# Reordering the DMA issues of a fused attention and spline-FFN kernel: an earlier input load, block moves ahead of other transfers, and a second issuing engine

## The chip, the cores and the metric

The kernel runs on one core of a Trainium2 chip. The metric is the device time of one execution in microseconds (us). Three runs of the kernel before gave 541.97, 543.44 and 547.85 us; their median, 543.44 us, is the time before. Engines are called PE (matrix multiplication), DVE (vector), ACT (scalar, activations), POOL (GpSimd) and SP (which here does nothing but issue DMAs).

## The reference

Everything is float32. `x` has 4 batches of 512 tokens of 512 features. A layer norm is shared by an attention of 16 heads (head size 32, ALiBi bias, causal mask) and by a gated FFN whose three weight matrices are dense samples of Catmull-Rom splines through a few control points.

```python
xn = _layernorm(x)
q, k, v = proj(xn, Wq, bq), proj(xn, Wk, bk), proj(xn, Wv, bv)
scores = einsum("bhqd,bhkd->bhqk", q, k) / sqrt(32) + alibi + causal_mask
attn = softmax(scores) @ v            # heads joined again, then @ Wo + bo
gate_w, up_w, down_w = (spline_reconstruct(cp) for cp in control_points)
inter = silu(xn @ gate_w.T) * (xn @ up_w.T)
out = x + attn + inter @ down_w.T
```

## The kernel before

The kernel has two stages. The first (to about 385 us) is the attention, with the preparation of the FFN's tables beside it; the second is the FFN, a sequence of plain steps that the change does not touch. The instruction order on each engine is the order in which the Python code writes it (`in_order`, L385), so the text of the main loop (L1104 to L1169) is the schedule.

**Units.** The attention is cut into 64 units `(b, hg, i)`: batch, group of four heads, query tile `i` of 128 queries. Four units with one `(b, hg)` are called a group here, numbered 0 to 15 (four groups a batch). Step `n` of the loop starts unit `n`; older units are in later phases. For a unit: PE makes the scores (L897); DVE adds the bias and finds minima (`minima`, L917); ACT takes exponentials with their sums (`exponentials`, L932); DVE takes reciprocals (L945) and POOL multiplies by them (`normalize`, L947).

**Turning the probabilities.** For the product with `v` the probabilities must lie with keys on partitions. Key tile 0 of query tiles 0 and 1 is transposed by PE (`turn`, L951). Everything else goes in two parts (`swap`, L963): DVE transposes 32x32 blocks into a tile `blocks0` or `blocks1` (L972), and then four DMAs, one for each 32 source partitions `a`, spread the blocks over partitions into one shared tile, called `moved` in the profile (`move`, L977 to L982). Query tile 1 has 4 moves of 64 KB, tile 2 4 of 192 KB, tile 3 4 of 256 KB. Tiles 1 and 3 share the buffer `blocks1` (`i % 2`): DVE can't write tile 3's blocks until tile 1's moves have landed, and not tile 1's of the next group until tile 3's have landed. `values` (L986) multiplies `moved` by `v` on PE (L1000), at step 3 of the next group; the next group's moves may not overwrite `moved` until that is done.

**Where the moves stand.** Within a step the order is: DVE and ACT work of the unit, the transposes of `swap`, spline-table arithmetic on DVE (`terms`, L1150), the lists `items[n]` and `small[n]` (projections, loads and so on, hung on a step by the code from L1022 to L1068), then the collected `moves` (L1157), then the deferred DMAs in `later` (`flush`, L1159), then table loads (L1163). At step 0 of a group the transposes of tile 2 (of the group that ended) come before the minima of the new tile 0 and 1, those of tile 3 after them; the moves of both come at the end of the step. Tile 1's are at step 3.

**Queues.** All DMAs but the table copies (POOL, L553) and a few rows of zeros are issued by SP, one after the other; SP waits in order. The framework gives the DMAs of SP and ACT eight completion semaphores in turn, so that a DMA also waits for the one eight before it to have landed.

**Other work on the queue.** `load_turned` (L806) loads the next batch's raw `x`, transposed, 1 MB, into one of two `xnT` buffers; it hangs on `items[at + 6]` (L1052), where `at` is the batch's first step. `norm_turned` (L810, DVE, L814) normalizes it in place from step `at + 8` on, with row statistics that come back through DRAM (`write_rows` L798, `read_rows` L804), and PE's `value` (L863) and projections (L827) need it from step `at + 10` on. `project_out` (L1026) spreads the output projection of the batch before: a load of `xT` into one of three `xt` buffers (L485, 256 KB) hangs on step `n - 2`, PE and DVE work on step `n` (L490, L497), and the result's store (L500) goes into `later`. `stepped` (L878) makes four small moves of `v` into `moved` (L884) once a batch.

Of the kernel before, what the change touches and what calls it, by code (L numbers as in the profile page):

```python
# [23 lines left out]
NB = D // P  # L24
# [376 lines left out]
def block_kernel(  # L401
# [18 lines left out]
    nc = tc.nc  # L420
# [52 lines left out]
    later = deque()  # L473

    def flush():
        while later:
            later.popleft()()

    def proj(b, r, pool, tag):

        xt = []

        def load():
            xt.append(xtp.tile([P, S], F32, name="xt"))
            nc.sync.dma_start(out=xt[0], in_=xT[b, r * P : (r + 1) * P, :])  # L485

        def go():
            ps = pool.tile([P, S], F32, name=tag)
            for c in range(NB):
                nc.tensor.matmul(  # L490
                    ps,
                    lhsT=wsb["o"][:, c, r * P : (r + 1) * P],
                    rhs=ctxT[b][:, c, :],
                    start=(c == 0),
                    stop=(c == NB - 1),
                )
            nc.vector.scalar_tensor_tensor(  # L497
                xt[0], ps, bocol[:, r : r + 1], xt[0], ALU.add, ALU.add
            )
            later.append(lambda: nc.sync.dma_start(out=mid[b][:, r], in_=xt[0]))  # L500

        return [load, go]
# [47 lines left out]
    def copy_rows(n):  # L550
        for _ in range(n):
            to, rows = copies.popleft()
            nc.gpsimd.dma_start(out=to, in_=rows)  # L553
# [31 lines left out]
    with ExitStack() as att:  # L585
# [216 lines left out]
        def read_rows(b):  # L802
            rows[b] = tp.tile([P, 2, S], F32, name="rows")
            nc.sync.dma_start(out=rows[b], in_=token[b].partition_broadcast(P))  # L804

        def load_turned(b):  # L806
            xnT[b] = xtp.tile([P, NB, S], F32, name="xnT", bufs=2)
            nc.sync.dma_start(out=xnT[b], in_=xn0[b].rearrange("(c p) s -> p c s", p=P))

        def norm_turned(b, t):  # L810
            at = slice(t * P, (t + 1) * P)
            for k, op in enumerate((ALU.subtract, ALU.mult)):
                own = rows[b][:, k, at].unsqueeze(1).to_broadcast([P, NB, P])
                nc.vector.tensor_tensor(xnT[b][:, :, at], xnT[b][:, :, at], own, op)  # L814
# [71 lines left out]
        units = [(b, hg, i) for b in range(B) for hg in range(NHG) for i in range(NB)]  # L886
# [76 lines left out]
        def swap(u):  # L963

            b, hg, i = u
            if i == 0:
                return lambda: None
            first = int(i < TURNED)
            at = slice(3 * i - 4 + first, 4 * i - 3)
            own = tp.tile([P, NB, i + 1 - first, NG, Q32], F32, name=f"blocks{i % 2}")  # L970
            for c in range(first, i + 1):
                nc.vector.transpose(  # L972
                    own[:, :, c - first].rearrange("p r j k -> p j r k"),
                    soft[u][0][:, :, c * P : (c + 1) * P].rearrange("p j (r k) -> p j r k", k=Q32),
                )

            def move():  # L977
                for a in range(NB):
                    nc.sync.dma_start(  # L979
                        out=blocks[:, a, at].rearrange("p s j k -> p (s j k)"),  # L980
                        in_=own[a * Q32 : (a + 1) * Q32].rearrange("p r s j k -> p r (s j k)"),
                    )  # L982

            return move
# [37 lines left out]
        items = {n: [] for n in range(len(units) + LAG)}  # L1022
# [3 lines left out]
        def project_out(b, spots):  # L1026
            for r, n in enumerate(spots):
                load, go = proj(b, r, *((ps_m, "mm") if n < len(units) else (ps_s, "s")))
                items[n - 2].append(load)
                (early if n % NB == NB - 1 else items)[n].append(go)  # L1030

        for b in range(B):
            at = 4 * NHG * b
            for hg in range(NHG):
                nb, nh = divmod(b * NHG + hg + 1, NHG)
                if nb < B:

                    items[at + 4 * hg - (b > 0 and hg == 1)].append(project("q", nb, nh))
                    items[at + 4 * hg + 1 + (b > 0 and hg == 1)].append(project("k", nb, nh))
            if b == 0:  # L1040
                items[0].pop()
                items[0], items[1] = items[1], []
                for n, t in ((1, 1), (2, 2), (3, 3)):
                    items[n].append(value(0, t))
            elif b < B - 1:
                project_out(b - 1, [at + n for n in (4, 5, 6, 7)])
            else:
                project_out(b - 1, [at + n for n in (10, 12, 14, 16)])
            if b + 1 < B:
                for t in range(NB):  # L1050
                    small[at + 8 + t].append(lambda b=b, t=t: norm_turned(b + 1, t))
                items[at + 6].append(lambda b=b: load_turned(b + 1))  # L1052
                small[at + 5].append(lambda b=b: write_rows(b + 1))
                items[at + 7].append(lambda b=b: read_rows(b + 1))
                for t, n in enumerate(((10, 11, 14, 15), (10, 11, 14, 15), (14, 18, 19, 22))[b]):
                    items[at + n].append(value(b + 1, t))
                for n, step in zip((1, 1, 2, 2, 3, 3, 3, 4, 4), stat_steps(b + 1)):
                    small[at + n].append(step)
                if b + 2 < B:
                    items[at + 11].append(lambda b=b: load_x(b + 2))  # L1060
        for b in range(B):
            at = 4 * NHG * b
# [41 lines left out]
        for n in range(len(units) + LAG):  # L1104
            u = units[n] if n < len(units) else None
            old = units[n - LAG] if n >= LAG else None
            if u and u[2] != 1:
                scores(u)
            moves = []
            if u and u[2] == 0:  # L1110
                if old and old[2] < TURNED:
                    turn(old)
                if n:
                    normalize(units[n - 1])
                    moves.append(swap(units[n - 2]))
                minima(u)
                minima(units[n + 1])
            else:
                if u and u[2] > 1:
                    minima(u, range(NG // 2))  # L1120
                if n <= len(units):
                    normalize(units[n - 1])
                if u and u[2] > 1:
                    minima(u, range(NG // 2, NG))
            for step in early[n]:
                step()
            keep_it = None
            if n % NB == NB - 1 and n >= NB + LAG:
                g = n // NB - 1
                keep_it = values(g // NHG, g % NHG)  # L1130
                exponentials(u, range(NG))
                keep_it()
            if old and old[2] < TURNED and not (u and u[2] == 0):
                turn(old)
            if u and not keep_it:
                exponentials(u, range(NG))
            if n % NB == 0 and n:
                if u is None:
                    moves.append(swap(units[n - 2]))
                moves.append(swap(units[n - 1]))  # L1140
            elif n % NB == NB - 1:
                moves.append(swap(units[n - 2]))
            assert n < 53 or done == len(terms)
            if n >= NB:
                credit = min(credit + TERMS[n % NB] - 0.3 * len(small[n]), 2.0)
            while done < len(terms) and credit > 0.0:
                cost, of, *term = terms[done]
                if of in due or of in fresh:
                    break
                nc.vector.tensor_tensor(*term)  # L1150
                done += 1
                credit -= cost
                if done in loads:
                    due[done] = loads[done]
            for step in (*items[n], *small[n]):
                step()
            for move in moves:  # L1157
                move()
            flush()  # L1159
            fresh = set()  # L1160
            if n % NB in (1, 2):
                for load in due.values():
                    load()  # L1163
                fresh = set(due)
                due.clear()
            if n >= 12:
                copy_rows(min(COPIES[n % NB], len(copies) - 2 * NB))
            if old:
                soft.pop(old)  # L1169
# [241 lines left out]
```

## Time and profile before

| | |
|---|---|
| median of three runs | 543.44 us (541.97 to 547.85) |
| profiled execution | 538.82 us |
| its span, first to last instruction | 537.0 us |
| mean granted PE clock | 0.974 |
| PE busy | 497.2 us (93%) |
| DVE / ACT / POOL busy | 366.8 / 267.7 / 255.2 us |
| moves of tile 1 / 2 / 3 | 64 each; 64 / 192 / 256 KB; median 3.1 / 3.7 / 4.8 us from issue to landing |

A row of the profile names the source line, the engine, the operation and the tiles as `out<-in`. "Idle before" is the time in which an engine did nothing just before the instruction, with the instruction or DMA whose end released it. In the timeline, `SPq` rows are DMA issues, and the second number is how long the issuing took. `PEclk` is the granted PE clock, 1.0 being full speed. The DMA share is the mean busy share of the 16 DMA engines.

### The profile page before, as it was taken

What the parts mean: (1) busy time and instruction counts of PE and PEld (TensorE: products, weight loads), DVE (VectorE), ACT (ScalarE), POOL (GpSimd) and SP (SyncE); (2) the same over time, 40 slices, a digit from 0 to 9 for tenths busy, and PEclk for the clock granted to TensorE, in tenths of its full rate; (3) what the DMA queues carried; (4) which work ended last, traced back from release to release, by engine and by line L of the source; (5) the groups of instructions that cost most, each with busy time, mean ns of one, the idle gap of its engine ahead of it and who ended that gap; (6) DMA issues with size and microseconds to landing.
All of it is one profiled execution on the core that took longest, in us unless ns stands there. A gap on an engine that the chain in (4) does not pass through costs nothing.

```text
span 537.0 us, 11697 instructions
## 1 busy us (share of the span) xinstructions
PE 497.2 (93%) x4092; PEld 240.0 (45%) x4092; DVE 366.8 (68%) x1023; ACT 267.7 (50%) x726; POOL 255.2 (48%) x441
## 2 busy tenths in 40 slices
PE   7999959998994999799998999978899999999997
PEld 5644414444441434344344444334334645746463
DVE  6069879879675997886887566684035584855836
ACT  2376646746361675544676756772214433624222
POOL 4025536848272974827567647673018233231310
PEclk9999979999997999799999999997999999999999
DMA  8925888979888787878868657886956566745344
GB/s 305 363 83 110 306 225 293 268 224 282 236 248 237 249 214 256 254 174 247 202 158 231 154 117 201 243 213 181 260 160 190 177 213 199 245 137 205 123 165 166
DMA packets 67522, 114.31 MB, mean 213 GB/s; under 512 B 10796, under 2 KB 29228, under 8 KB 66952
## 3 DMA queue, kind: packets, MB, share of 16 engines
q1 hardware_dynamic: 62600, 105.08, 66.6%
q0 software_dynamic: 4864, 8.49, 5.4%
q8 instruction: 32, 0.52, 0.4%
q14 instruction: 26, 0.21, 0.1%
HBM read 54.27 MB, written 23.70 MB: 145 GB/s over the span
## 4 chain that ended last, share of the span: by engine, by line
PE 59%; DMA 14%; DVE 14%; SPq 6%; issue 4%; ACT 2%; POOL 1%; DVEq 0%; ACTq 0%
PE mm L827 12%; PE g L568 9%; PE mm L863 6%; DMA moved<-blocks 6%; PE o L1283 6%; DVE blocks L972 5%; PE c L1000 5%; PE s L897 4%; SPq L979 4%; PE o L1229 4%; DVE p L917 4%; PE o L1300 3%; PE o L490 3%; PE mm L490 3%; DMA xt<-in_xT_dram 2%
## 5 line engine op out<-in xcount | busy, mean ns | idle before, releaser
L947 POOL TENSOR_SCALAR p<-p,inv 128x128 f32<-128x128 f32 (+3 forms) x256 | 155.6, 621 | 156.2 <-DVE inv L945 154.8
L932 ACT ACTIVATE p<-p,low 128x128 f32<-128x128 f32 (+3 forms) x256 | 140.4, 551 | 82.2 <-DVE low L917 77.9
L917 DVE CUSTOM_DVE_ANT_0 p<-s,dist 128x128 f32<-128x128 f32 (+3 forms) x256 | 109.9, 480 | 49.0 <-PE s L897 48.9
L972 DVE STREAM_TRANSPOSE blocks<-p 128x512 f32<-128x512 f32 x128 | 81.1, 681 | 27.5 <-DMA moved<-blocks 26.4
L1205 POOL COPY made<-inner 128x512 f32<-128x512 f32 x64 | 38.8, 635 | 104.1 <-DVE inner L1204 66.1
L863 PE MATMUL mm<-wv,xnT 128*128 128x512 f32 x128 | 62.7, 634 | 14.0 <-issue 13.0
L568 PE MATMUL g<-feat,wT 32*64 32x512 f32 x832 | 61.7, 592 | 0.0
L1197 ACT ACTIVATE act<-g 128x512 f32<-128x512 f32 x60 | 31.0, 602 | 58.9 <-PE g L568 58.6
L827 PE MATMUL mm<-xnT,wq 128*128 128x512 f32 (+1 forms) x136 | 57.9, 569 | 1.0 <-DVE xnT L814 0.7
L827 PE MATMUL mm<-xnT,wk 128*128 128x512 f32 (+1 forms) x136 | 58.1, 570 | 0.2 <-ACT xnT L778 0.2
L897 PE MATMUL s<-kT,qT 32*128 32x512 f32 (+3 forms) x512 | 52.1, 468 | 2.3 <-DVE low L917 2.2
L932 ACT ACTIVATION_READ_ACCUMULATOR p<-p,low 128x1 f32 x256 | 48.2, 188 | 0.0
L1000 PE MATMUL c<-moved,v 128*32 128x256 f32 (+2 forms) x512 | 34.2, 412 | 14.7 <-DMA xt<-in_xT_dram 5.7
L863 PEld LDWEIGHTS mm<-wv,xnT 128*128 128x128 f32 x128 | 24.6, 203 | 44.2 <-issue 39.6
L490 PE MATMUL mm<-ctxT,wo 128*128 128x512 f32 x88 | 39.7, 597 | 0.0
L1204 DVE TENSOR_TENSOR inner<-g,act 128x512 f32<-128x512 f32 x40 | 24.8, 683 | 21.7 <-PE g L568 10.7
L827 PEld LDWEIGHTS mm<-xnT,wk 128*128 128x128 f32 x136 | 25.5, 190 | 29.5 <-issue 27.5
L568 PEld LDWEIGHTS g<-feat,wT 32*64 32x64 f32 x832 | 28.9, 131 | 21.1 <-issue 9.9
L897 PEld LDWEIGHTS s<-kT,qT 32*128 32x128 f32 x512 | 21.4, 184 | 35.3 <-issue 16.4
L553 POOL DMA_DIRECT2D table<-samples x64 | 36.7, 579 | 0.0
L827 PEld LDWEIGHTS mm<-xnT,wq 128*128 128x128 f32 x136 | 24.8, 190 | 24.5 <-issue 22.0
L1283 PE MATMUL o<-inner,dRM 32*64 32x512 f32 x512 | 34.9, 588 | 0.0
(114 smaller groups left out, 588.8 us busy)
## 6 DMA issues: line engine op xcount, KB each, us to landing
moved<-blocks SPq DMA_DIRECT2D x64, 256.0 KB, 4.8
moved<-blocks SPq DMA_DIRECT2D x64, 192.0 KB, 3.7
feat<-table SPq DMA_DIRECT2D x16, 512.0 KB, 4.7
inner<-made SPq DMA_DIRECT2D x32, 256.0 KB, 4.5
table<-samples POOLq DMA_DIRECT2D x64, 88.0 KB, 4.8
xp<-in_xp_dram SPq DMA_DIRECT2D x16, 256.0 KB, 4.6
feat<-in_coef_dram SPq DMA_DIRECT2D x8, 512.0 KB, 5.4
feat<-in_rowpts_dram SPq DMA_DIRECT2D x8, 512.0 KB, 8.0
```

Source lines behind the costliest of these rows:

```text
L490: nc.tensor.matmul(ps, lhsT=wsb["o"][:, c, r * P : (r + 1) * P], rhs=ctxT[b][:, c, :], start=(c == 0), stop=(c == NB - 1),)
L568: nc.tensor.matmul(ps[k][cols, :], lhsT=wT[rows, q, 2 * w + part, cols], rhs=feat[b][rows, q, part, :], start=(part == 0), stop=(part == 1),)
L827: nc.tensor.matmul(ps[0][:, tokens], lhsT=wsb[name][:, c, hg * P : (hg + 1) * P], rhs=xnT[b][:, c, tokens], start=(c == 0), stop=(c == NB ...
L863: nc.tensor.matmul(ps[0], lhsT=xnT[b][:, c, t * P : (t + 1) * P], rhs=wsb["v"][:, c, :], start=(c == 0), stop=(c == NB - 1),)
L897: nc.tensor.matmul(banks[b, hg][j][:, at : at + (k + 1) * P], lhsT=qk[b, hg, "q"][rows, k * P : (k + 1) * P], rhs=qk[b, hg, "k"][rows, : ( ...
L917: nc.vector.tensor_tensor_reduce(out=p[:, j, :nk], in0=ps[j], in1=own, scale=-SLOPES[hg * NG + j], scalar=BIG, op0=ALU.add, op1=ALU.min, a ...
L932: nc.scalar.activation(p[:, j, :nk], p[:, j, :nk], AF.Exp, bias=low[:, j : j + 1], scale=-1.0, accum_out=total[:, j : j + 1],)
L947: nc.gpsimd.tensor_scalar(p[:, j, :nk], p[:, j, :nk], inv[:, j : j + 1], 1.0, ALU.mult, ALU.mult)
L972: nc.vector.transpose(own[:, :, c - first].rearrange("p r j k -> p j r k"), soft[u][0][:, :, c * P : (c + 1) * P].rearrange("p j (r k) -> ...
L1000: nc.tensor.matmul(ps[j * HD : (j + 1) * HD, to], lhsT=v(j), rhs=part(j), start=(c == 0), stop=(c == NB),)
L1205: nc.gpsimd.tensor_copy(made[:, k], four[:, k])
L1283: nc.tensor.matmul(sums[b][r][cols, :], lhsT=dR[rows, a, cols], rhs=o[rows, :], start=(a == 0), stop=False,)
```

## The change

Four edits in the attention's schedule; no arithmetic changes, and PE, DVE and POOL carry the same instructions in the same order.

1. `load_turned(b + 1)` hangs on step `at + 2` (`at + 3` for the first batch) and not on `at + 6`.
2. The load of `xT` in `project_out` goes into `later`, so that it is issued after the moves of its step.
3. At step 0 of a group the moves of tile 2 are issued at once, ahead of whatever DMAs the step's `items` issue.
4. Of tile 3's four moves, those with `a` = 1 and 3 are issued by ACT; SP keeps 0 and 2. On ACT they stand behind the exponentials of tile 0 and the query projection's copy (L839) and ahead of the exponentials of tile 1.

```diff
@@ swap
             def move():
                 for a in range(NB):
-                    nc.sync.dma_start(
+                    queue = nc.scalar if i == NB - 1 and a % 2 else nc.sync
+                    queue.dma_start(
                         out=blocks[:, a, at].rearrange("p s j k -> p (s j k)"),
                         in_=own[a * Q32 : (a + 1) * Q32].rearrange("p r s j k -> p r (s j k)"),
                     )
@@ project_out
-                items[n - 2].append(load)
+                items[n - 2].append(lambda load=load: later.append(load))
@@ the lists of a batch
-                items[at + 6].append(lambda b=b: load_turned(b + 1))
+                items[at + 2 + (b == 0)].append(lambda b=b: load_turned(b + 1))
@@ the main loop, step 0 of a group
-                    moves.append(swap(units[n - 2]))
+                    swap(units[n - 2])()
```

## The prediction

> **What bounds the kernel now.** I read the page first (engines, clock, chain), then who waited for whom, then the timeline around the two longest waits, then the DMA share by stretches.
>
> ```profile
> PE 497.2 (93%) x4092; PEld 240.0 (45%) x4092; DVE 366.8 (68%) x1023; ACT 267.7 (50%) x726; POOL 255.2 (48%) x441
> PEclk9999979999997999799999999997999999999999
> ```
>
> PE is the bound: only 537.0 - 497.2 = 39.8 us of the span are not PE work, and four slices have a reduced clock. A gain can only come from these 39.8 us and from the slow-clock stretches. The waits on PE, and one on DVE, say where they are:
>
> ```profile
> PE mm L863 <- issue: 13.0, 2, 6.8
> PE c L1000 <- DMA xt<-in_xT_dram: 5.7, 2, 4.5
> PE c L1000 <- issue: 5.5, 4, 1.8
> PE c L1000 <- DMA moved<-blocks: 1.9, 2, 1.3
> PE c L1000 <- DMA mid<-xt: 1.5, 1, 1.5
> ...
> DVE blocks L972 <- DMA moved<-blocks: 26.4, 8, 6.4
> ```
>
> Two waits of `value` take 13.0 us. Waits of `values` for tile 3's moves take 5.7 + 5.5 + 1.9 + 1.5 = 14.6 us in nine pieces (where "issue" or another DMA is named, it is still `moved` that L1000 reads). The two long ones have one cause:
>
> ```profile
> 57.81 0.45 SPq L808 DMA_DIRECT2D xnT<-in_xn_dram  x1
> 63.46 14.28 SPq L979 DMA_DIRECT2D moved<-blocks  x12
> 71.08 2.49 DVE L972 STREAM_TRANSPOSE blocks<-p 128x512 f32<-128x512 f32 x4 [3.61 <-DMA moved<-blocks]
> 73.49 1.37 DVE L814 TENSOR_TENSOR xnT<-xnT,rows 128x512 f32<-128x512 f32 x2
> 74.97 5.84 PE L863 MATMUL mm<-wv,xnT 128*128 128x512 f32 x8 [6.13 <-issue]
> ...
> 153.16 0.40 SPq L808 DMA_DIRECT2D xnT<-in_xn_dram  x1
> 158.42 4.46 SPq L979 DMA_DIRECT2D moved<-blocks  x4
> 167.11 2.49 DVE L972 STREAM_TRANSPOSE blocks<-p 128x512 f32<-128x512 f32 x4 [6.40 <-DMA moved<-blocks]
> 171.00 5.61 PE L863 MATMUL mm<-wv,xnT 128*128 128x512 f32 x8 [6.84 <-issue]
> ```
>
> In groups 1 and 5 the 1 MB load of `x` stands ahead of tile 1's moves. Those land late, DVE waits with tile 3's transposes (same buffer), `norm_turned` stands behind them on DVE, and PE's `value` needs it. What the DMA engines do:
>
> ```profile
> core 0: us, PE busy (x) PEld busy (x) DVE busy (x) ACT busy (x) POOL busy (x), PEclk, DMA share, GB/s
> 31.00:42.00 11.00, 11.00 (x40) 4.27 (x38) 7.43 (x26) 7.75 (x23) 4.11 (x8) 1.00 0.00 1
> 57.00:70.00 13.00, 11.80 (x84) 5.74 (x80) 8.71 (x30) 9.21 (x30) 4.97 (x8) 1.00 0.99 349
> 118.00:138.00 20.00, 18.28 (x113) 8.07 (x110) 15.93 (x58) 12.34 (x39) 12.99 (x23) 1.00 0.92 273
> 153.00:166.00 13.00, 11.15 (x76) 5.18 (x68) 6.15 (x23) 6.80 (x22) 4.74 (x8) 1.00 0.98 331
> ```
>
> DMA is full where the load stands now, empty at 31 to 42 us, and nearly full at 118 to 138 us.
>
> **Part 1, x sooner, batch 1.** The load moves from step 6 to step 3. SP has issued all its earlier work by 25.3 us and next issues at 41.4, so the load runs in the empty stretch; its 0.45 us of issue and its transfer cost nothing (cover: the idle DMA to 42 us). At 57 to 70 us a full queue loses 1 MB: 1.05 MB / 349 GB/s = 3.0 us. Tile 1's moves, tile 3's transposes, L814 and `value` come 3.0 us sooner; DVE is free for it from 67.4 us. The 6.13 us wait becomes 3.1. The clock then decides: from 70.5 to 77.3 us the granted clock was 0.65, and the eight matmuls took 5.84 us where eight take 3.6 elsewhere, 2.2 lost. If that stretch stays, all eight fall into it and lose up to 3.6, 1.4 more (gain 1.6); if it goes, the gain is 5.2. I take 2.5.
>
> **Part 1, batch 2.** The load goes from 153.2 us to right behind group 3's tile 3 moves, about 118.3 us. There the share is 0.92: of 1 MB (3.8 us at 273 GB/s) about a third fits in the free 1.6 us of these 20, and the rest delays tile 1's moves of group 4 by up to 2.2 us. DVE already waited 4.33 us for them (transposes at 138.68). Two us later, minima of tile 2 end at 149.2 instead of 147.2, and the scores of tile 3, which PE started at 147.3, follow them: PE loses 1.0 (0 to 3). In group 5 three things come off: 1 MB / 331 GB/s = 3.2 us of queue; SP's stop at 150.86 to 154.46, where a table load needed the semaphore of the `xt` load (they no longer share it); and 2 us of SP's issuing before the store at 145.84, as ACT issues two of the moves. Tile 1's moves then land near 160 us instead of 167, which is when DVE has finished its minima (160.7); L814 follows at 163 to 164, and PE's k projection and scores run until 164.2. The 6.84 us wait closes to about 1.0: gain 5.8, and 2.0 of slow clock (5.61 against 3.6 us; the clock was 0.65 from 166 to 172.9), which a wait of 1 us should not bring on: of the seven PE waits of 1.2 to 1.8 us only that at 215 us was followed by a slow stretch. Together -5.8 - 2.0 + 1.0 = -6.8 (from -8.8 to 0: the queue's 3.2 us alone, less 3 in group 4).
>
> **Part 1, batch 3.** The load comes ahead of tile 1's moves issued at 224.2. With 3.8 us (their row's median is 3.1) they would land at 231; tile 3's transposes ran at 232.9. Hidden, 0 (to +1 if the cover is short).
>
> **Parts 2 and 3, order on SP.** Where the step has other DMAs, tile 2's moves now come first: in group 4 an `xt` load and four `v` moves (134.7 to 138.4 us, waiting for table loads), in group 12 the `v` moves (310.5 to 313.3). What is moved behind, `xt` and `v`, is needed two steps and a group later. PE worked throughout in group 4, so nothing is gained; group 12 had a 0.77 us wait, which goes. In groups 13 and 14 one `xt` load each (256 KB, 0.8 us at 303 to 349 GB/s) stood before tile 2's moves, and there `values` waited 1.25 and 4.48 us. Gain 0.8 + 0.8 + 0.8 = 2.4 (0 to 3). The store of the first row of `project_out` now precedes a load that may wait for it; SP stopped there before too (145.84 to 150.86).
>
> **Part 4, two issuers: the transfer.** The trace has no ACT-issued DMA. From SP the four take 0.54, 0.60, 1.44 and 1.30 us (374.2 to 378.3), and `values` starts at 382.46.
>
> ```profile
> L979 SPq DMA_DIRECT2D moved<-blocks x192: 542/603/1718, 41.4 to 377.0; - x192
> 375.20:376.40 1.20, 1.20 (x20) 1.00 0.77 108
> 376.40:378.20 1.80, 1.80 (x10) 1.00 0.96 170
> 378.20:379.20 1.00, 1.00 (x8) 1.00 0.92 303
> ```
>
> The engines are 0.96 busy at 170 GB/s, so SP's later issues take long because the transfers do; saving issue time saves no landing time. But one move alone runs at 108 GB/s and the boundary between moves at 303: each reads only 32 partitions. If a mix runs better, 1 MB takes less and up to 14.6 - 2.4 = 12.2 us of `values` waits go; if not, 0, or a loss where SP's next loads now share the engines with ACT's half. I take 0, as the 0.96 row is the nearest. [...]
>
> **Part 4: ACT.** ACT now waits, ahead of tile 1's exponentials, for tile 3's transposes, in nearly every group (it was ready before they ended in groups 0 to 14), then issues: two issues are 0.54 + 0.60 = 1.15 us, at worst 1.2 + 1.7 = 2.9. Behind it: tile 1's exponentials (1.97 us), the copy of k, tile 2's exponentials; and DVE's reciprocal of tile 1, which stands between the minima of tile 2. That reciprocal came 4.6 us after the transposes' end in group 1 (73.6 to 78.3), enough for 1.15 + 1.97 = 3.1. It came 0.9 us after in group 12 (320.0 to 320.9) and 1.6 in group 14 (354.8 to 356.4): DVE loses 2.2 and 1.5 there, and under 0.6 in groups 6 and 10. PE is covered by projections until 325.6 in group 12, and waits for moves in group 14 anyway. I take +1.0 (0 to +10, below).
>
> **Sum:** -2.5 - 6.8 - 2.4 + 0 + 1.0 = -10.7. The profiled execution took 538.8 (span 537.0 and 1.8 around it), so 528.1; it ran 4.6 below the median of the runs, so I forecast 543.4 - 10.7 = 532.7 us.
>
> **Rivals.** (a) The jam only moves: group 4 loses the whole 3 us, and group 5 gains only its 3.2. For it: 0.92 share at 118 to 138; against: the semaphore stop and SP's two us go as well. -2.5 + 0 - 1.0 + 1.0 = -2.5: 541 us. (b) Slower: ACT in front of its DMAs. If the two issues cost 2.9 us, tile 1's exponentials end 4.9 us after the transposes, past the reciprocal in 12 of 15 groups; DVE's losses by the timeline's gaps add up to about 18. If all reach PE, 18 - 9.3 (part 1) = +9: 552 us. It decides where two issues take over 1.5 us. Against: SP's first two issues take 1.15 even with a full queue, and PE has projections to do. (c) Pairs of moves run faster: 8 of the 12.2 us more, 525 us. [...]
>
> **How the numbers follow.** Chances: forecast 0.45 (own range 529 to 538), (a) 0.25, (b) 0.15, (c) 0.15. About 1% (5.4 us) is what a measurement of this kernel tells from no change; below 538.0 is faster, above 548.9 slower. Faster: nearly all of the forecast (0.43), (c), a tenth of (a): 0.60. Slower: (b), 0.15. Same: 0.25. Range 523 to 548: from (c) with a little more, past (a); it leaves out (b) and the end of (c), under 0.2.
>
> **What would show it.** Right: no wait over 3.5 us before L863; tile 3's transposes of group 5 without a wait for `moved`; group 4's wait 4.3 to 6.5 us; `values` waits at 10 to 14 us. Wrong: ACT issues of L980 above 1.5 us for two, DVE waiting for ACT before L945, PE before the scores for DVE; or `values` waits under 6 us, which would be (c).

## The result, and the profile after

Over 12 runs each, the changed kernel took 546.31 us (median; 543.42 to 548.90) against 541.06 us (536.96 to 547.85): a ratio of 1.0107, 95% interval 1.0075 to 1.0139. It is slower by about 1%, where 532.7 us had been forecast; that was counted from 543.4 us, the median of the first three runs, and the same -10.7 us from 541.06 would be 530.4. The ratios here and below leave out executions more than 1.5% above the fastest of the same kernel (545.26 and 547.85 us here, of the kernel before), and so need not be the quotient of the medians. The profiled execution took 543.4 us, with a span of 541.6 against 537.0.

The engine and clock lines of the page of the changed kernel:

```profile
PE 509.9 (94%) x4092; PEld 246.2 (45%) x4092; DVE 366.7 (68%) x1023; ACT 266.1 (49%) x726; POOL 256.0 (47%) x441
PEclk9999979998999999699999999988799999999999
```

PE's time outside its work fell from 39.8 to 31.7 us, yet PE was busy 12.7 us longer with the same 4092 matmuls. It lost less by waiting and more at a reduced clock: 35.0 us of its work fell into stretches at half clock (granted 0.50 to 0.51), where it was 18.8 before, which makes about 8 of the 12.7 us; the other 4 to 5 us were not traced. Who waited for whom in the changed kernel (columns: sum in us, times, longest; line numbers are one higher than before from L979 on):

```profile
DVE inv L945 <- ACT p L932: 14.0, 14, 3.0
DVE blocks L972 <- DMA moved<-blocks: 10.9, 7, 2.9
DVE xt L497 <- DMA xt<-in_xT_dram: 10.3, 3, 4.8
...
PE c L1001 <- DMA moved<-blocks: 5.3, 4, 2.3
```

DVE's wait for `moved` fell from 26.4 to 10.9 us. Part 1 was meant to do this, but by itself it leaves 21.8 (run 1 below); in groups 1 and 5, its aim, the wait fell from 3.6 to 1.1 and from 6.4 to 2.9 us. Two waits of DVE that were 2.7 and 2.6 us are new in size: for ACT's exponentials (14.0) and for the loads of `xt` (10.3). The two `value` rows of groups 1 and 5 in the timeline of the changed kernel:

```profile
72.61 6.73 PE L863 MATMUL mm<-wv,xnT 128*128 128x512 f32 x8 [2.84 <-DVE inv L945]
...
167.31 3.67 PE L863 MATMUL mm<-wv,xnT 128*128 128x512 f32 x8 [0.98 <-DVE inv L945]
```

Group 5 came out as written down: a wait of 0.98 us and eight matmuls in 3.67 us at full clock. In group 1 the wait fell to 2.84, and most of the time of the eight matmuls fell into a stretch at half clock (71.9 to 78.7 us). To see where the gain went, compare, group by group, when `values` starts on the matmuls that read tile 3's moves (worked out from both traces, after minus before): group 1 -1.5 us, group 4 +2.2, group 5 -2.9, group 9 -1.2, group 13 -1.0, group 14 +1.8, group 15 +5.2. Gains of groups 1 and 5 are given back in groups 2 to 4 and 7 to 10, and 6.2 us are lost in the last two groups.

The median time from issue to landing of tile 3's 256 KB moves, first the kernel before, then the changed one (size, median us):

```profile
moved<-blocks SPq DMA_DIRECT2D x64, 256.0 KB, 4.8
```

```profile
moved<-blocks SPq DMA_DIRECT2D x32, 256.0 KB, 7.1
moved<-blocks ACTq DMA_DIRECT2D x32, 256.0 KB, 7.4
```

With two issuers each move is issued sooner and is under way for half as long again. The trace has the landing of few of these moves (18 of 64 before, 8 of 64 after), so the medians are rough; run 3, with 18 of 64, has 6.4 and 7.0 us.

### The profile page after: what moved, and what is told of

It is laid out like the page before. It is cut to its first block, busy times and chain, and to the rows that moved or that the text cites. A ratio compares the mean times of both kernels' runs of the same rounds, so it can differ in the third digit from the quotient of the medians.

```text
span 541.6 us, 11694 instructions
## 1 busy us (share of the span) xinstructions
PE 509.9 (94%) x4092; PEld 246.2 (45%) x4092; DVE 366.7 (68%) x1023; ACT 266.1 (49%) x726; POOL 256.0 (47%) x441
## 3 DMA queue, kind: packets, MB, share of 16 engines
q10 hardware_dynamic: 4608, 8.39, 7.7%
## 4 chain that ended last, share of the span: by engine, by line
PE 58%; DMA 20%; DVE 13%; SPq 3%; ACT 3%; issue 2%; ACTq 1%; POOL 0%; DVEq 0%; POOLq 0%
DMA moved<-blocks 10%; PE mm L827 9%; PE g L568 9%; DVE blocks L972 7%; PE o L1284 6%; PE mm L863 5%; PE mm L490 5%; PE c L1001 5%; PE o L1230 4%; DVE p L917 3%; PE s L897 3%; PE o L1301 3%; PE o L490 3%; DMA xt<-in_xT_dram 3%; ACT p L932 2%; SPq L980 2%
## 5 line engine op out<-in xcount | busy, mean ns | idle before, releaser
L972 DVE STREAM_TRANSPOSE blocks<-p 128x512 f32<-128x512 f32 x128 | 81.1, 681 | 12.8 <-DMA moved<-blocks 10.9
L1206 POOL COPY made<-inner 128x512 f32<-128x512 f32 x64 | 38.8, 634 | 101.7 <-DVE inner L1205 79.2
L897 PE MATMUL s<-kT,qT 32*128 32x512 f32 (+3 forms) x512 | 58.7, 476 | 5.8 <-DVE low L917 5.5
L568 PE MATMUL g<-feat,wT 32*64 32x512 f32 x832 | 63.5, 591 | 0.0
L1001 PE MATMUL c<-moved,v 128*32 128x256 f32 (+2 forms) x512 | 36.0, 428 | 9.8 <-DMA moved<-blocks 5.3
L897 PEld LDWEIGHTS s<-kT,qT 32*128 32x128 f32 x512 | 24.2, 185 | 41.5 <-DVE low L917 15.4
L568 PEld LDWEIGHTS g<-feat,wT 32*64 32x64 f32 x832 | 30.1, 131 | 20.5 <-issue 10.2
L1284 PE MATMUL o<-inner,dRM 32*64 32x512 f32 x512 | 36.8, 588 | 0.0
```

The costliest lines, as they stand in the source:

```text
L568: nc.tensor.matmul(ps[k][cols, :], lhsT=wT[rows, q, 2 * w + part, cols], rhs=feat[b][rows, q, part, :], start=(part == 0), stop=(part == 1),)
L897: nc.tensor.matmul(banks[b, hg][j][:, at : at + (k + 1) * P], lhsT=qk[b, hg, "q"][rows, k * P : (k + 1) * P], rhs=qk[b, hg, "k"][rows, : ( ...
L972: nc.vector.transpose(own[:, :, c - first].rearrange("p r j k -> p j r k"), soft[u][0][:, :, c * P : (c + 1) * P].rearrange("p j (r k) -> ...
L1001: nc.tensor.matmul(ps[j * HD : (j + 1) * HD, to], lhsT=v(j), rhs=part(j), start=(c == 0), stop=(c == NB),)
L1206: nc.gpsimd.tensor_copy(made[:, k], four[:, k])
L1284: nc.tensor.matmul(sums[b][r][cols, :], lhsT=dR[rows, a, cols], rhs=o[rows, :], start=(a == 0), stop=False,)
```

## The experiments

Two theories stood at the start. T: part 2 costs, since DVE waits for late `xt` in the last batch. R: part 4 costs, since ACT issues in front of its exponentials. Each ratio is to the kernel before on the same chip, and stands with its 95% interval.

**1. Part 1 alone.**

```diff
-                items[at + 6].append(lambda b=b: load_turned(b + 1))
+                items[at + 2 + (b == 0)].append(lambda b=b: load_turned(b + 1))
```

> Part 1 alone (the load of turned x moved, the rest as before). Both theories: group 1's wait before L863 falls from 6.13 to about 3 us, group 5's from 6.84 to about 1. Theory T (the change loses by its late loads of xt) expects 3 to 6 us less, a ratio of 0.989 to 0.995 to the kernel before. Theory R (it loses by ACT issuing moves in front of its exponentials) expects the same or better, since nothing of ACT's is touched: 0.985 to 0.995. If it comes out at 1.000 or above, part 1 itself is worth nothing here, and the waits that it closed came back elsewhere, as slow clock or as a wait in group 4.

Measured: 537.02 against 541.76 us, 0.991 (0.9875 to 0.9945), a gain of 4.9 us by the ratio. The waits fell to 3.48 us in group 1 and 3.35 in group 5, but the eight matmuls behind them took 6.50 and 6.51 us:

```profile
73.90 6.50 PE L863 MATMUL mm<-wv,xnT 128*128 128x512 f32 x8 [3.48 <-DVE inv L945]
169.44 6.51 PE L863 MATMUL mm<-wv,xnT 128*128 128x512 f32 x8 [3.35 <-DVE inv L945]
```

In group 4 DVE's wait with tile 3's transposes grew from 4.3 to 6.5 us, as the prediction had reckoned. Over the whole profile PE's waits of over 0.25 us fell from 35.7 to 29.8 us and its busy time rose by 6.4. Part 1 pays, and the clock keeps a share: its mean was 0.967 in the profiled execution, where it was 0.974.

**2. Part 2 alone.**

```diff
-                items[n - 2].append(load)
+                items[n - 2].append(lambda load=load: later.append(load))
```

> Part 2 alone (the loads of xt issued behind the moves of their step). T: DVE's waits before L497 for the load of xt grow from 2.6 us to 8 or more, the last two groups end 4 to 7 us later, ratio 1.008 to 1.013. R: DVE has slack before L497, ratio 0.998 to 1.002.

Measured: 548.57 us, 1.0108 (1.0059 to 1.0157). It costs by itself what the whole change costs, as T says.

**3. Part 4 alone.**

```diff
-                    nc.sync.dma_start(
+                    queue = nc.scalar if i == NB - 1 and a % 2 else nc.sync
+                    queue.dma_start(
```

> Part 4 alone (ACT issues two of tile 3's four moves). T: DVE waits for ACT's exponentials before L945 by some 10 us in all, as in the changed kernel (14.0), but PE mostly has other work: ratio 1.000 to 1.005. R: those waits reach PE through the minima and scores: ratio 1.010 to 1.018.

Measured: 551.09 us, 1.0176 (1.0128 to 1.0225). R's number, and more than part 2's. T is wrong in calling part 4 cheap, R in calling part 2 free.

**4. The changed kernel without part 2.** The edit of 2 is undone.

> The changed kernel with part 2 undone (loads of xt ahead of the moves again; parts 1, 3 and 4 kept). T: DVE's waits before L497 fall back to about 3 us and the last two groups get back 4 to 7 us: ratio 0.995 to 1.002 to the kernel before, against 1.011 for the changed kernel. R: 1.006 to 1.012, nearly as slow as the changed kernel.

Measured: 547.09 us, 1.0066 (1.0023 to 1.0108). In company part 2 is worth only 1.0107 - 1.0066 = 0.4 points, with intervals of ±0.3 and ±0.4: R's number. Beside part 4, part 2 costs little, at most some 0.9 points by these intervals.

**5. The changed kernel without part 4.** The edit of 3 is undone.

> The changed kernel with part 4 undone (SP issues all of tile 3's moves; parts 1, 2 and 3 kept). The first runs gave parts alone 0.991 (part 1), 1.011 (part 2) and 1.018 (part 4), so neither T nor R holds alone. If the prices add, part 4 off the changed kernel (1.011) leaves 0.993 to 1.000. If parts 2 and 4 delay the same work in the last two groups (T), most of part 2's price stays: 1.000 to 1.006. If part 4 is what costs (R), 0.988 to 0.995.

Measured: 541.70 us, 1.002 (0.9985 to 1.0056). The price of part 4 in company is 0.9 points. Parts 1 and 2 alone multiply to 1.002, which leaves nothing for part 3 within some 0.7 points. `values` is 3.9 us ahead in group 13 and 4.3 behind in group 15: here too the loss is in the last two groups, and DVE's wait for `xt` is the cause that the profile names:

```profile
DVE xt L497 <- DMA xt<-in_xT_dram: 21.8, 4, 8.7
```

In the changed kernel, where only two of tile 3's four moves stand ahead of the load on SP, it is 10.3 us.

**6. Part 2 in the last batch only.**

```diff
-                items[n - 2].append(load)
+                items[n - 2].append((lambda load=load: later.append(load)) if b == B - 2 else load)
```

> Part 2 alone, and only for the four loads of xt in the last batch (the eight of the two batches before stay ahead of the moves). T: the price is that of late rows in the last batch, where DVE waits before L497: ratio 1.007 to 1.013, as with all twelve (1.011). Rival: the price is spread, one wait of DVE in the second batch (group 4) and one later are half of it: 1.002 to 1.007. If it is 1.000 or less, the loads of the early batches cost it all.

Measured: 548.07 us, 1.0135 (1.009 to 1.018): the four loads of the last batch carry all of the price. The third of them, first in the kernel before and then here (timeline rows):

```profile
350.26 0.59 SPq L485 DMA_DIRECT2D xt<-in_xT_dram  x1
358.06 0.75 DVE L497 SCALAR_TENSOR_TENSOR xt<-mm,bcol,xt 128x512 f32<-128x512 f32 x1 [0.60 <-PE mm L490]
```

```profile
363.70 1.67 SPq L485 DMA_DIRECT2D xt<-in_xT_dram  x1
370.96 0.75 DVE L497 SCALAR_TENSOR_TENSOR xt<-mm,bcol,xt 128x512 f32<-128x512 f32 x1 [9.73 <-PE c L1000]
```

The load's step is a step 0 of a group, and tile 3's moves go out in that step. Behind them, the load waits for tile 3's transposes and for SP to issue four moves (4.13 us here). It goes out 13.4 us later, 3.8 of them brought along from the group before (tile 3's transposes end 3.8 us later, and the first late load had DVE wait 3.76 us at L497, where it had waited 1.59); DVE stands at L497 for 9.73 us (the row names PE's `values`, long irrelevant to L497; what L497 lacked was `xt`, landing 7 us after its issue). Right behind L497 on DVE stand the minima of group 15's tile 3, at 371.63 where they were at 359.11. `values` of group 15 starts 10.0 us later than before. In all, DVE's waits for late `xt` are 9.7 + 6.7 = 16.4 us, where they were 2.6.

**7. Part 4 with one move by ACT** (otherwise as 3).

```diff
+                    queue = nc.scalar if i == NB - 1 and a == NB - 1 else nc.sync
```

> Part 4 alone with one move by ACT (the last, a = 3), SP keeps three. If ACT's time of issue is what costs (2.1 to 2.4 us for two, of which the first takes 0.6), a single issue leaves a quarter to a half of the price: 1.003 to 1.009. If it is that ACT must wait for tile 3's transposes ahead of tile 1's exponentials, the price stays: 1.013 to 1.020.

Measured: 534.76 us, 0.9896 (0.9865 to 0.9927). Neither expectation: one move by ACT makes the kernel faster by 1%, two make it slower by 1.8%.

**8. ACT's wait without its issues.**

```diff
+                if i == NB - 1:
+                    nc.scalar.copy(stat.tile([P, 1], F32, name="seen"), own[:, 0, i - first, 0, 0:1])
                 for a in range(NB):
                     nc.sync.dma_start(
```

> The kernel before, with all moves issued by SP, and one copy of 128x1 on ACT that reads the last block of tile 3's transposes, at the place where part 4 has ACT issue: it puts the wait there without the DMA issues (the copy itself is under 0.3 us, 15 times). If the wait costs, 1.010 to 1.020; if the time of issuing does, 1.000 to 1.004.

Measured: 540.16 us, 0.9986 (0.9952 to 1.0019). The wait that part 4 puts on ACT costs nothing.

**9. ACT's wait and lost time, with no DMA of ACT's.** As 8, with twelve copies into a tile of 128x12.

> SP issues all the moves; ACT waits for tile 3's transposes and then is busy with twelve copies of 128x1 (0.19 us each by the run with one copy, 2.3 us together, as long as its two issues) ahead of tile 1's exponentials. That run, wait and one copy alone, gave 0.999. If ACT's lost time is part 4's price (1.018 alone), this shows it with no DMA of ACT's: ratio 1.010 to 1.020. If the price is in the queues (two issuers that hold each other up, transfers in another order), 0.998 to 1.004.

Measured: 539.17 us, 0.9971 (0.9941 to 1.0001). The row shows that the edit did less than it was meant to do, since the copies, listed at 0.19 us each, overlap:

```profile
214.22 1.22 ACT L981 COPY seen<-blocks 128x1 f32<-128x1 f32 x12 [1.55 <-DVE blocks L972]
```

Twelve take 1.22 us, and not 2.3. So 1.2 us of ACT's time cost nothing; for the 2.4 us of two issues see 16.

**10. ACT's issues parted.** A list `held` keeps the move `a` = 3 until the end of step 1, behind tile 1's exponentials.

```diff
+                    if i == NB - 1 and a == NB - 1:
+                        held.append(lambda: send(nc.scalar, NB - 1))
+                    else:
+                        send(nc.scalar if i == NB - 1 and a == 1 else nc.sync, a)
...
+            if n % NB == 1:
+                while held:
+                    held.pop()()
```

> Part 4 alone with ACT's two issues parted: a = 1 at its place, a = 3 only behind tile 1's exponentials. If the price is ACT's time ahead of tile 1's exponentials (one issue there gave 0.990, two 1.018), it goes: 0.988 to 1.000. If two moves through ACT's queue cost wherever they are issued, or the later landing of a = 3 is what values waits for, 1.005 to 1.020.

Measured: 551.72 us, 1.0178 (1.0138 to 1.0219). DVE's wait for ACT before L945 fell to 5.5 us, and the time stayed where it was. R falls: the price doesn't go with ACT's time.

**11. Other pairs** (otherwise as 3). SP issues `a` = 0 and 1, ACT 2 and 3, so that 0 goes beside 2 and 1 beside 3: "far" pairs, where 3 has the "near" ones, 0 beside 1 and 2 beside 3.

```diff
+                    queue = nc.scalar if i == NB - 1 and a >= 2 else nc.sync
```

> Part 4 alone with ACT issuing a = 2 and 3 (source partitions 64 to 127) and SP a = 0 and 1, so that the two queues read different halves of the partitions at a time. If part 4 is dear because the pairs 0 with 1 and 2 with 3 share the same half, this is cheaper than 1.018: 1.000 to 1.010, and ACT's second issue is shorter than 1.5 us. If it is ACT's time or the number of issues, it stays: 1.012 to 1.022, second issue 1.4 to 1.8 us.

Measured: 546.92 us, 1.0103 (1.0059 to 1.0148), with ACT's second issue still at 1.7 us in most groups. Which halves the two queues read at a time is worth 0.7 points; the intervals overlap (1.0128 to 1.0225 in 3).

**The new theories.** Timeline rows of group 7, around the moves of tile 3, for the kernel before, for two moves by ACT (3), and for one (7):

```profile
213.30 4.18 SPq L979 DMA_DIRECT2D moved<-blocks  x4
217.52 0.60 SPq L685 DMA_DIRECT2D feat<-in_downtab_dram  x1
...
221.79 2.79 PE L1000 MATMUL c<-moved,v 128*32 128x256 f32 x20 [1.66 <-issue]
```

```profile
218.59 2.37 ACTq L980 DMA_DIRECT2D moved<-blocks  x2
218.62 1.19 SPq L980 DMA_DIRECT2D moved<-blocks  x2
219.85 1.65 SPq L685 DMA_DIRECT2D feat<-in_downtab_dram  x1
221.54 3.41 SPq L685 DMA_DIRECT2D feat<-in_downpts_dram  x1
...
229.20 0.65 PE L1001 MATMUL c<-moved,v 128*32 128x256 f32 x4 [2.10 <-DMA feat<-in_downtab_dram]
```

```profile
213.85 0.59 ACTq L980 DMA_DIRECT2D moved<-blocks  x1
213.88 2.49 SPq L980 DMA_DIRECT2D moved<-blocks  x3
216.41 1.73 SPq L685 DMA_DIRECT2D feat<-in_downtab_dram  x1
...
221.52 2.86 PE L1001 MATMUL c<-moved,v 128*32 128x256 f32 x32
```

With four moves on SP the next table load is issued 4.2 us after the first move, with three 2.6, with two 1.3. Those loads are less urgent than the moves: DVE waits 2.1 us in all for `feat` in the kernel before. `values` starts on the moves 8.5, 7.7 and 10.6 us after the first issue. This gives theory S: SP, free too soon, puts its next loads beside ACT's half of the moves. Against it Q: two queues move the four moves more slowly, whatever else runs.

**12. SP held until ACT's first move has landed.**

```diff
+                if i == NB - 1:
+                    seen = stat.tile([P, 1], F32, name="seen")
+                    nc.sync.dma_start(out=seen[0:1], in_=blocks[0:1, 1, at][:, 0, 0, 0:1])
```

> Part 4 alone (1.018), and SP held back: behind its two moves SP issues a DMA of four bytes that reads what ACT's first move (a = 1) writes, so that SP's next load is issued only when that move has landed, some 4 to 5 us after the transposes' end, about where it was before (4.2), and not at 1.3. Theory S (SP's next loads are issued sooner and share the DMA engines with ACT's half of the moves): the price goes, ratio 0.990 to 1.003, and the time from the transposes' end to values, summed over 16 groups, falls from 132.5 to under 124 us. Rival Q (two queues move the four moves more slowly, whatever else runs): 1.010 to 1.020, the sum stays above 128.

Measured: 550.99 us, 1.0198 (1.016 to 1.0236): by the time, Q's number. But the hold was longer than meant:

```profile
222.92 1.19 SPq L980 DMA_DIRECT2D moved<-blocks  x2
229.22 0.64 SPq L986 DMA_DIRECT2D seen<-moved  x1
229.91 0.38 SPq L685 DMA_DIRECT2D feat<-in_downtab_dram  x1
```

SP went on 7 us after its first move, not 4, and what it loads came late in its turn: DVE's waits for `feat` grew from 2.1 to 7.9 us. The time leaves S and Q open.

**13. Three moves by ACT** (`queue = nc.scalar if i == NB - 1 and a else nc.sync`).

> Part 4 alone with three moves by ACT (a = 1, 2, 3) and one by SP, which is free for its next load some 0.7 us after the transposes' end. S: three moves instead of two share with that load, ratio 1.018 to 1.035. Rival: the price goes with the two moves of a pair that run at the same time, not with SP's next load; three in one queue are again one after the other: 0.990 to 1.010.

Measured: 572.78 us, 1.0571 (1.0523 to 1.062). SP's next load goes out 0.7 us after the transposes, and the price is three times that of two moves, above S's range. DVE's waits for ACT before L945 are 38.8 us here, so ACT's issues may have a share in it.

**14, 15, 16. A shorter hold, its control, and the other halves.** At the head of step 1 SP issues a DMA of four bytes that waits for tile 1's second exponential: on the kernel before (`hold0`), on 3 (`hold4`) and on 11 (`hold4_far`).

```diff
+            if u and n % NB == 1 and n > NB:
+                seen = stat.tile([P, 1], F32, name="seen")
+                nc.sync.dma_start(out=seen[0:1], in_=soft[u][2][0:1, 1:2])
```

> Control: the kernel before, and SP issues a DMA of four bytes, at the head of step 1 of each group, that reads the second head's sum of tile 1's exponentials, so that the loads of that step come no sooner than ACT has got there. SP was busy with tile 3's moves until 4.2 us after the transposes' end anyway: 0.997 to 1.006 by both theories.

> Part 4 alone (1.018) with that hold: ACT issues until 2.4 us after the transposes' end, its second exponential ends near 3.4, and SP's next load is issued at some 4 us, not at 1.3. S: 0.990 to 1.004, and the sum over the groups from the transposes' end to values falls from 132.5 to under 125 us. Q: 1.010 to 1.020, sum above 128.

> As hold4, with a = 2 and 3 by ACT and 0 and 1 by SP, so that the two moves under way at a time read different halves of the partitions (without the hold 1.010). S: as hold4, 0.990 to 1.004. Q with the shared half as its cause: below hold4 by about the 0.007 that the halves were worth without the hold, 1.003 to 1.012.

Measured: hold0 543.45 us, 1.0053 (1.0024 to 1.0083); hold4 545.88 us, 1.0106 (1.0071 to 1.0141); hold4_far 540.07 us, 1.0015 (0.9982 to 1.0049). By its raw ratio hold4 is in Q's range. But the hold itself costs 0.5 points, as the control shows; against the control, two moves by ACT cost 0.5 points and not 1.8, and with the far halves nothing (0.4 below the control, each interval being ±0.3). The control is taken to cost the same in all three; its DMA also takes one of the eight semaphores in turn (before, SP's 478 DMAs signal eight, 59 or 60 each), and what that changes was not told apart.

**The yardstick was wrong, too.** The expectations of 12 and 14 count to the first matmul of `values`. By that count the sum is 132.5 us in 3, 136.2 in 12, 129.0 in hold4 and 129.7 in hold4_far: above 128, as Q had said, and not under 125, as S had. But that matmul works on what PE turned itself (L961) and waits for no move of tile 3. The count that follows was thus chosen after the runs. Counted to the first matmul that reads tile 3's moves (L1001, `c<-moved,v`), summed over 16 groups, one profiled execution each:

| kernel | SP's next DMA after the transposes, group 7 | transposes' end to moves read | ratio |
|---|---|---|---|
| before | 4.3 us | 145.3 us | 1 |
| hold0 | 4.4 | 145.6 | 1.0053 |
| wait only (8) | as before | 145.9 | 0.9986 |
| one move by ACT (7) | 2.6 | 137.7 | 0.9896 |
| two, near pairs (3) | 1.3 | 158.7 | 1.0176 |
| two, far pairs (11) | 1.3 | 149.2 | 1.0103 |
| two parted (10) | 1.3 | 161.0 | 1.0178 |
| three (13) | 0.7 | 178.4 | 1.0571 |
| two, SP held to landing (12) | 6.4 | 148.7 | 1.0198 |
| two, hold4 | 3.6 | 147.0 | 1.0106 |
| two, hold4_far | 3.5 | 140.7 | 1.0015 |

The sum follows S. With one move by ACT all four are issued by 2.6 us instead of 4.2, and SP's next load still stands behind three of them: 7.6 us less. With two and three SP is free sooner still, and the sum rises by 13.4 and 33.1 us; the hold takes 11.7 of the 13.4 away (158.7 to 147.0). The DMA packets in the traces say the same without any matmul. ACT's moves have a queue of their own (q10 of the page of 3: 8.39 MB). The times from the transposes' end to the last packet of this queue add up over the groups to 137.5 us in 3, 125.7 in hold4, and 116.5 in 12, where SP loaded nothing until ACT's first move had landed. Other queues moved 0.83, 0.70 and 0.45 MB a group (median) meanwhile; SP's own half of the moves is 0.5 MB. The pairs count beside it: far instead of near takes 9.5 us off without the hold and 6.3 with it. In 12 the moves were as quick as in hold4, and the loss came back elsewhere: from the end of one group's `values` to the end of the next group's transposes the sum rose from 155.3 to 167.2 us. So S holds for most of part 4's price (1.8 points without the hold, 0.5 with it against the control; without the control, 0.7 of the 1.8), a smaller part belongs to the pairs, and Q as "whatever else runs" falls: in 12 ACT's queue is done 21.0 us sooner, with SP's loads kept back. R, for two moves, falls with 10 and with hold4_far. ACT issues both moves there ahead of its exponentials, DVE waits for them as follows (first the kernel before, then hold4_far), and the kernel is level with the one before:

```profile
DVE inv L945 <- ACT p L932: 2.7, 5, 0.5
```

```profile
DVE inv L945 <- ACT p L932: 21.1, 15, 3.6
```

Moves that are read sooner (140.7 against 145.6 us in the control) may have paid for some of these waits, so that a small price is not excluded. For three moves R and S were not parted.

**17, 18. What paid, put together.** Part 1 and one move by ACT; the second version has part 3 too.

> A version made of what paid alone: part 1 (0.991) and one move of tile 3 by ACT (0.990). If they act in different places (part 1 in groups 1 and 5, the move in the rest), the gains add: 0.980 to 0.985. If the single move gained through the same two jams, or what it gained is within the spread, 0.986 to 0.992.

Measured: 530.20 against 540.74 us, 0.9816 (0.9775 to 0.9858). The page:

```profile
PE 501.1 (95%) x4092; PEld 240.4 (46%) x4092; DVE 366.6 (69%) x1023; ACT 266.9 (51%) x726; POOL 254.7 (48%) x441
PEclk9999989999997999799999999998999999999999
```

The span is 527.5 us: PE's time outside its work is 26.4 us where it was 39.8, with PE's busy time up by 3.9. The gains add (0.991 x 0.9896 = 0.981). This version beats both kernels.

> Parts 1 and 3 and one move by ACT. Without part 3 this gave 0.982. Parts 1, 2 and 3 together gave 1.002 where 0.991 and 1.011 multiply to 1.002, so part 3 should add nothing: 0.978 to 0.986. If tile 2's moves ahead of the loads are worth the 0.8 us a group that was forecast for three groups (2.4 us), 0.976 to 0.979.

Measured: 532.88 against 541.34 us, 0.9852 (0.9808 to 0.9896). Part 3 adds nothing; whether it costs 0.4 points is within the intervals.

## Why the prediction was wrong, point by point

- **Part 1, forecast -2.5 and -6.8 us.** The mechanism was right: both waits of `value` shrank (6.1 to 2.8 and 6.8 to 1.0 us in the changed kernel), since tile 3's transposes of groups 1 and 5 waited less for `moved`, and group 5's matmuls ran without a slow stretch. The size was too large: -4.9 us alone. In part 1 alone group 5 kept a wait of 3.35 us, and its eight matmuls took 6.51 us. And in the changed kernel group 4 gave back more than the 1.0 us allowed: from group 1 to group 4 `values` lost 3.7 us, near the 3 us of rival (a). How much of that is part 1's load and how much part 4 was not told apart; part 1 alone lost 2.3 us over the same groups.
- **Parts 2 and 3, forecast -2.4 us: the step that failed.** It reads "What is moved behind, `xt` and `v`, is needed two steps and a group later", and so priced the delay at nothing, and a gain of 2.4 us beside it. For `xt` two steps were all the cover there was. In two of the last batch's four steps the load fell behind tile 3's moves, which themselves wait for the transposes, and it went out 10 and 13 us late (6). Measured: +5.9 us alone by the ratio, against -2.4; part 3 nothing. The prediction asked for each wait what is queued behind it on its engine, but not for `xt`: L497 stands on DVE ahead of the minima of tile 3.
- **Part 4, the transfer, forecast 0: the second step that failed.** The text named the loss, "where SP's next loads now share the engines with ACT's half", and took 0 all the same, since the engines were 0.96 busy. Busy engines were the reason to fear it: with two moves by ACT the time from the transposes' end to the moves read rose from 145.3 to 158.7 us, and 11.7 us of that went when SP's loads were held. By the ratio part 4 costs +9.5 us alone, and 0.9 points in company. Runs 14 to 16 and the DMA packets show that most of it is this sharing: held back, SP's loads leave 0.5 of the 1.8 points.
- **The pairs.** The forecast set no price on which halves are read at a time. The runs show one: near pairs cost 0.7 points more than far ones without the hold (1.0176 against 1.0103), 0.9 with it (1.0106 against 1.0015); why was not shown. And where the prediction said that "saving issue time saves no landing time", that saving (4.2 to 1.3 us of SP) is what did most of the harm, because of what SP issued with it.
- **Part 4, ACT, forecast +1.0, and rival (b), 552 us.** (b) ended on the right side for another reason. Its threshold was passed (two issues 2.4 us, 14.0 us of DVE's waits for ACT), yet ACT's wait and 1.2 us of ACT's time cost nothing (8, 9), and 21.1 us of DVE's waits stand in a kernel that is no slower (hold4_far). Losses on DVE were added up as if PE had to pay them.
- **Rival (c), 525 us,** is not borne out for the pairs as they were split (13.4 us slower in the sum). One move by ACT beside three by SP did run quicker, 7.6 us in the sum and 1% of the time, and far pairs behind the hold were 4.9 us quicker than the control. The 303 and 108 GB/s that spoke for it were no clean pair: 18 of the 77 packets in the window of 108 are still of tile 2's moves (1536 bytes), and the window of 303 opens when nearly all four moves of tile 3 have been issued.
- **The clock.** It was priced for the two waits of `value` alone; all else was priced at the length of the wait. The changed kernel waits 8 us less and is busy 12.7 us more, about 8 of them by work at half clock. The prediction also read the clock in windows that lie 2 us early: the stretches behind the two waits run from 72.5 to 79.3 and from 168.1 to 174.9 us, at 0.50, and the 0.65 is a mean with full speed ahead of them.

What stays open: why parts 2 and 4 together cost less than their product (1.0107 against 0.991 x 1.0108 x 1.0176 = 1.019); that they delay the same work in the last two groups fits 4 and 5, and so does that part 4 takes half of the moves out of the way of `xt` (21.8 us of DVE's waits for it in 5, 10.3 in the changed kernel), but neither was tried by itself. Nor was it tried to keep far pairs and change the order of SP's loads without a hold DMA.

## What to carry to other kernels

Here SP, busy with urgent transfers, also kept the less urgent ones back: its next DMA went out 4.3 us after the transposes with four moves, 1.3 with two. Before taking work from an issuer, ask what it will issue in the time it gains and which transfers that will slow (145.3 to 158.7 us from the transposes' end to the moves read). A load put behind other transfers inherited their waits: in 6 it went out 13.4 us later, behind four moves whose issuing took 4.13 us. So count what the transfers ahead of a load wait for, and not their bytes alone. A new wait on an engine off the path is a price only where the path is shown to pay it: here a kernel with 21.1 us of DVE waiting for ACT, where it had been 2.7, was level.

## What the runs showed that was not expected

- Moving one of four 256 KB transfers to a second issuer gained 1.0%, two lost 1.8%, three lost 5.7%.
- A DMA's issue on ACT took 0.59 us (median), the second right behind it 1.7 us, while two issues on SP took 1.19 us and SP's next two 1.65 and 3.41 us (run 3, group 7). In the kernel before, behind four moves on SP, the same two took 0.60 and 0.94 us.
- Twelve copies of 128x1 on ACT, each listed at 0.19 us, took 1.22 us together (run 9, group 7).
- A DMA of four bytes per group in SP's queue, waiting where SP had just become free anyway, cost 0.5% (hold0, 1.0024 to 1.0083).
